# Layer 0's state turned between steps by DVE blocks and DMA through DRAM, with three smaller moves and a new rule of order, in a statically ordered graph kernel

## The chip, the cores and the metric

One core of a Trainium2 chip. Its engines are named as in the profile: PE is TensorE (products and transposes; PEld are its weight loads), DVE the vector engine, ACT the scalar engine, POOL is GpSimd, and SP (SyncE) issues the DMAs. PSUM is the memory that TensorE writes; ACT or DVE copies from there. The metric is device time of one execution in microseconds. The kernel before takes 1832.0 us (median of 4 runs, 1831.1 to 1833.3).

Ratios compare the mean time of one kernel's runs with the mean of the other's runs of the same rounds on the same chip, so they are not quite the ratio of the medians quoted beside them.

## The reference, cut

64 graphs of 256 nodes and 128 features, all float32, pass four layers, each with a residual and a layer norm. The parts that matter:

```python
# layer 0: a gated recurrent step, five times, with one adjacency matrix
def step(h, _):
    m_in = jnp.einsum('nm,bmd->bnd', in_matrix, h)          # needs h by nodes
    m_out = jnp.einsum('nm,bmd->bnd', out_matrix, h)
    av = jnp.concatenate([m_in, m_out], axis=-1)
    u3 = h @ u3_w.T + u3_b                                   # needs h by features
    z = jax.nn.sigmoid(av @ w3_w.T + w3_b + u3)
    r = jax.nn.sigmoid(av @ w4_w.T + w4_b + u3)
    hv = jnp.tanh(av @ w5_w.T + w5_b + (r * h @ u5_w.T + u5_b))
    h = (1.0 - z) * h + z * hv
# layer 2: attention; s_dst is needed as a row, the same on every partition
scores = s_src[:, :, None] + s_dst[:, None, :]
# every layer
x = _layernorm(x + layer(x), axis=-1)
```

A step makes the new state with features on partitions, and the next step's first product needs it with nodes on partitions as well. That turn, four times per pair of graphs, is what the change moves.

## The kernel before, the parts concerned

The kernel records every operation with its reads, writes, engine and an assumed duration. A list scheduler then fixes **one static order for each engine's queue** and assigns buffers. An engine waits at the head instruction of its queue, and what stands behind waits too: in the stall at 805 us below, a copy that ACT could have made from 803.6 us on was made at 806.59.

```python
SEEN = {"PE": 0.3, "ACT": 0.15, "DVE": 0.15, "POOL": 0.2, "SP": 2.5}
ABREAST = 4
...
# which ready operation comes next: earliest start, then oldest pair, then longest rest
key = (start + (us if len(op.ways) > 1 else 0.0), min(op.pair, self.n_pairs - ABREAST), -op.rest, op.number)
...
def transposes(i, x_like):                 # 4 TensorE transposes into PSUM
    ...
def to_sbuf(t, name):                      # PSUM copy, on ACT or DVE as the scheduler likes
    v = Value("A", name=name)
    evacuate(lambda: v.at(512), lambda: t.at(512), 0.6, 0.68, [t], [v])
    return v

def layer_norm(y, o):
    s, mv, rs = stats(y)                   # DVE statistics, then GpSimd: rs = (var + eps)**-0.5
    def fn():
        for c in range(4):
            nc.vector.tensor_scalar(tokens(o)[:, c, :], tokens(y)[:, c, :], mv()[:, c, 0:1], rs()[:, c:c + 1],
                                    op0=ALU.subtract, op1=ALU.mult)
    dve(1.4, fn, [y, s], [o])

def layer0(x0):
    hT = to_sbuf(transposes(x0, tokens), "hT")
    h = x0
    for s in range(STEPS):
        mT = to_sbuf(spread(h, aT), "mT")  # h is the stationary operand of this product
        ...                                # gates; the new state comes out as hT
        t = transposes(hT, lambda v: v.at(4, P))
        if s < STEPS - 1:
            h = to_sbuf(t, "h")

# layer 2: the score row, on every partition, by one 512-column product
pe(mm(512), lambda: nc.tensor.matmul(sd.at(512), vdst.ap, xT.at(512), start=True, stop=True), [vdst, xT], [sd])
```

## Time and profile before

| | before |
|---|---|
| time, median | 1832.0 us |
| TensorE busy | 1741 us, 95% |
| next engines | DVE 65%, ACT 43% |
| TensorE work by passes | 1700 us |
| not work: 0 to 200, 200 to 1600, from 1600 us on | 12, 50, 71 us |

"Work by passes" is the number of TensorE passes of each width times the start-to-start time of such a pass at full clock in the timeline (0.429 us for 512 columns, 0.216 for 256, 0.112 for 128, 0.110 for a transpose). What is left of a stretch is called its loss here: idle time, time at the halved clock, and passes that start later than they could. The lines are in the prediction.

### The profile page before, as it was taken

How to read it: one execution, taken by the hardware profiler on the slowest of the kernel's cores; microseconds unless marked ns; L12 is line 12 of the kernel's file. 1: busy time of each engine (PE TensorE's matmuls, PEld its weight loads, DVE VectorE, ACT ScalarE, POOL GpSimd, SP SyncE). 2: the span in 40 equal slices, each digit the busy share in tenths (PEclk: the TensorE clock that was granted, in tenths of full speed). 3: DMA queues.
4: the chain of work that ended last, by engine and by line, in shares of the span. 5: the costliest groups of instructions: out<-in, count | busy, mean ns of one | idle time of the engine just before them, and what ended most of it. 6: DMA issues, size and time to landing. Idle time of an engine off the chain costs nothing. (4 is left out here: it accounts for less than half of the span.)

```text
span 1832.3 us, 22228 instructions
## 1 busy us (share of the span) xinstructions
PE 1741.1 (95%) x7856; PEld 1230.3 (67%) x7856; DVE 1194.5 (65%) x3536; ACT 793.5 (43%) x1586; POOL 438.8 (24%) x519
## 2 busy tenths in 40 slices
PE   8999999999999999999999999999999999998767
PEld 6567576767767667676776666666766667665566
DVE  5466666667767667667776577665667666665753
ACT  3444445444445454434444444444444444443322
POOL 0022212312231221222222212231123222111152
PEclk9999999999999999999999999999999999999778
DMA  4000000000000000000000000000000000000000
GB/s 119 1 1 12 12 12 1 12 12 13 7 12 7 18 6 7 12 13 11 8 13 12 13 12 1 12 12 7 7 0 7 6 7 7 6 1 6 1 1 24
DMA packets 35024, 20.50 MB, mean 11 GB/s; under 512 B 1248, under 2 KB 34528, under 8 KB 34912
## 3 DMA queue, kind: packets, MB, share of 16 engines
q1 hardware_dynamic: 34912, 19.08, 3.6%
q8 instruction: 61, 1.00, 0.2%
q14 instruction: 51, 0.42, 0.1%
HBM read 10.69 MB, written 8.39 MB: 10 GB/s over the span
## 5 line engine op out<-in xcount | busy, mean ns | idle before, releaser
L173 ACT COPY a<-ps 128x512 f32<-128x512 f32 (+1 forms) x532 | 278.5, 541 | 483.5 <-PE ps L400 286.0
L419 POOL TENSOR_SCALAR s<-s 128x4 f32<-128x4 f32 x160 | 49.5, 310 | 986.1 <-DVE s L416 986.1
L400 PE MATMUL ps<-aT,a 128*128 128x256 f32 x1024 | 242.8, 379 | 1.7 <-ACT a L173 1.6
L400 PEld LDWEIGHTS ps<-aT,a 128*128 128x128 f32 x1024 | 189.9, 190 | 49.5 <-issue 24.5
L422 POOL TENSOR_TENSOR s<-s,neg_half 128x4 f32<-128x4 f32 x192 | 200.4, 1044 | 15.9
L430 DVE TENSOR_SCALAR x<-a,s 128x128 f32<-128x128 f32 x384 | 120.9, 370 | 100.1 <-POOL s L422 99.9
L462 DVE TENSOR_TENSOR a<-a,a 128x512 f32<-128x512 f32 x160 | 121.0, 756 | 95.4 <-ACT a L460 95.2
L460 ACT ACTIVATE a<-ps,bzrh 128x512 f32<-128x512 f32 x160 | 109.9, 687 | 160.6 <-PE ps L458 160.5
L446 ACT ACTIVATE a<-ps,bzrh 128x512 f32<-128x512 f32 x160 | 109.4, 685 | 160.1 <-PE ps L443 156.8
L448 DVE SCALAR_TENSOR_TENSOR a<-a,a 128x512 f32<-128x512 f32 x160 | 120.9, 759 | 81.1 <-ACT a L446 80.5
L414 DVE BATCH_NORM_STATS2 s<-a 128x6 f32<-128x128 f32 x640 | 141.5, 279 | 47.9 <-ACT a L173 45.7
L450 PE MATMUL ps<-a,w 128*128 128x512 f32 x320 | 163.0, 600 | 7.2 <-ACT a L446 7.0
L458 PE MATMUL ps<-a,u5h 128*128 128x512 f32 x320 | 164.4, 595 | 4.9 <-DVE a L448 4.9
L443 PE MATMUL ps<-a,w 128*128 128x512 f32 x320 | 163.6, 593 | 1.8 <-ACT a L173 1.8
L457 PE MATMUL ps<-a,w 128*128 128x512 f32 x320 | 164.5, 596 | 0.0
L442 PE MATMUL ps<-a,W 128*128 128x512 f32 x320 | 163.9, 594 | 0.0
L481 PEld LDWEIGHTS ps<-W,a 128*128 128x128 f32 x1024 | 131.7, 196 | 36.6 <-issue 17.9
L481 PE MATMUL ps<-W,a 128*128 128x128 f32 x1024 | 135.6, 281 | 8.7 <-DVE a L488 4.4
L452 ACT ACTIVATE a<-ps,bzrh 128x512 f32<-128x512 f32 x160 | 110.0, 688 | 62.7 <-PE ps L450 61.3
L400 PE MATMUL ps<-aT,x 128*128 128x256 f32 x512 | 129.3, 391 | 8.1 <-DVE x L430 7.7
L463 DVE SCALAR_TENSOR_TENSOR a<-a,a 128x512 f32<-128x512 f32 x160 | 118.5, 745 | 16.3 <-ACT a L452 13.9
L382 PEld LDWEIGHTS ps<-ident,a 128*128 128x128 f32 x768 | 92.4, 142 | 53.3 <-issue 23.2
(140 smaller groups left out, 2645.6 us busy)
## 6 DMA issues: line engine op xcount, KB each, us to landing
x<-x_in SPq DMA_DIRECT2D x32, 256.0 KB, 2.8
y_out<-a SPq DMA_DIRECT2D x32, 256.0 KB, 2.3
W<-mats_in SPq DMA_DIRECT2D x1, 832.0 KB, 6.7
W<-mats_in SPq DMA_DIRECT2D x1, 512.0 KB, 3.7
rbc<-rows_in SPq DMA_DIRECT2D x1, 385.0 KB, 7.2
aT<-adjT_in SPq DMA_DIRECT2D x1, 256.0 KB, 4.7
a<-adj_in SPq DMA_DIRECT2D x1, 256.0 KB, 5.9
ccol<-cols_in SPq DMA_DIRECT2D x1, 6.0 KB, 3.5
```

Of the source, the lines that this page charges most:

```text
L173: S.add([("ACT", us_act, lambda: nc.scalar.copy(o(), i())), ("DVE", us_dve, lambda: nc.vector.tensor_copy(o(), i()))], r, w)
L400: nc.tensor.matmul(t.at(2, N)[:, b, :], tokens(i)[:, 2 * b + j, :], right.ap[:, j, :], start=(j == 0), stop=(j == 1))
L414: nc.vector.bn_stats(st.at(4, 6)[:, c, :], tokens(y)[:, c, :])
L422: pool(1.04, lambda: nc.gpsimd.tensor_tensor(rs(), rs(), neg_half.ap, op=ALU.pow), [s, neg_half], [s])
L430: nc.vector.tensor_scalar(tokens(o)[:, c, :], tokens(y)[:, c, :], mv()[:, c, 0:1], rs()[:, c:c + 1], op0=ALU.subtract, op1=ALU.mult)
L442: nc.tensor.matmul(t.at(512), mat("u3"), hT.at(512), start=True, stop=False)
L443: nc.tensor.matmul(t.at(512), w345.ap[:, 1, :], mT.at(512), start=False, stop=True)
L450: pe(mm(512), lambda t=t, mT=mT: nc.tensor.matmul(t.at(512), w345.ap[:, 0, :], mT.at(512), start=False, stop=True, skip_group_check=True), ...
L457: nc.tensor.matmul(t.at(512), w345.ap[:, 2, :], mT.at(512), start=True, stop=False)
L458: nc.tensor.matmul(t.at(512), u5h.ap, r.at(512), start=False, stop=True)
L462: dve(0.7, lambda hv=hv, hT=hT: nc.vector.tensor_sub(hv.at(512), hv.at(512), hT.at(512)), [hv, hT], [hv])
L481: nc.tensor.matmul(tokens(t)[:, c, :], i.at(4, P)[:, c, :], w(), start=(k == 0), stop=(k == len(lefts) - 1))
```

## The change

The intent was to take everything from TensorE that is not arithmetic. In the words of its author, "the same, and layer 0's state is turned between its steps by DVE blocks and DMA through DRAM". Against the kernel before, the diff holds five things:

1. **Turn through DRAM**, for 28 of 32 pairs: DVE transposes 32x32 blocks, a store and four loads put the blocks in place. The spread then reads its weights at a step of four floats.
2. **First state arranged**: x is also loaded in its transposed layout (made on the host).
3. **Score row through DRAM**: a small DVE transpose and two DMAs in place of a product.
4. **Layer norms on ACT or DVE**, with one more small product on DVE between GpSimd and the normalizing.
5. **Order by deadlines**: 50 us apart, the last seven pairs 10 us apart.

Beside these the diff renews some assumed durations (2.5 to 3.3 us for a DMA, 0.70 to between 0.72 and 0.76 us for some DVE operations) and the numbers of buffers. Both bear on the order.

```diff
-SEEN = {... "SP": 2.5}
+SEEN = {... "SP": 3.3}
+DUE, LAST_DUE, LAST = 50.0, 10.0, 7
...
+    def tile(self, t):
+        return self.ap[:, t:512:4] if self.moved else self.ap[:, t * P:(t + 1) * P]
...
-                    key = (start + ..., min(op.pair, self.n_pairs - ABREAST), -op.rest, op.number)
+                    key = (start + ..., self.due(op.pair) - op.rest, op.number)
...
+        load(lambda: hTs[p].at(2, N), xT[2 * p:2 * p + 2].rearrange("b d n -> d b n"), hTs[p])
...
+    def turn_by_dma(i, name):
+        st, d, o = Value("A", name="turn"), Value("E", name="turn"), Value("A", name=name)
+        dve(1.11, lambda: nc.vector.transpose(st.ap.rearrange("p (b l t) -> p t b l", b=4, l=32), i.blocks()), [i], [st])
+        S.add([("SP", 0.45, lambda: nc.sync.dma_start(d.ap, st.ap))], [st], [d])
+        def move():
+            for f in range(4):
+                nc.sync.dma_start(o.ap[32 * f:32 * f + 32].rearrange("r (b n) -> r b n", b=4),
+                                  d.ap[:, f * P:(f + 1) * P].rearrange("(b r) n -> r b n", b=4))
+        S.add([("SP", 1.8, move)], [d], [o])
...
+        dve(0.16, lambda: nc.vector.scalar_tensor_tensor(nmr(), mv()[:, :, 0], -1.0, rs(), ...), [s], [s])
+        S.add([("ACT", 1.85, by_act), ("DVE", 1.45, by_dve)], [y, s], [o])
...
-            t = transposes(hT, lambda v: v.at(4, P))
-            if s < STEPS - 1:
-                h = to_sbuf(t, "h")
+            if s < STEPS - 1 and S.pair < n_pairs - BY_PE:      # BY_PE = 4
+                h = turn_by_dma(hT, "h")
+            else:
+                ...
...
-        pe(mm(512), lambda: nc.tensor.matmul(sd.at(512), vdst.ap, xT.at(512), ...), [vdst, xT], [sd])
+        dve(0.34, lambda: nc.vector.transpose(srow.at(4, 32), hs()[:, :, D - 30:D + 2]), [h], [srow])
+        S.add([("SP", 0.45, lambda: nc.sync.dma_start(line([32, 4], [P, 4], [1, 32]), srow.at(4, 32)[31::32]))], [srow], [d], 3.2)
+        S.add([("SP", 0.45, lambda: nc.sync.dma_start(sd.at(512), line([0, P], [1, 512])))], [d], [sd], 5.5)
```

## The prediction

> **What bounds the kernel now.** I read the page's busy shares first, then its slices, the windows of the steady part and of the end, TensorE's timeline, and its waits.
>
> ```profile
> span 1832.3 us, 22228 instructions
> PE 1741.1 (95%) x7856; PEld 1230.3 (67%) x7856; DVE 1194.5 (65%) x3536; ACT 793.5 (43%) x1586; POOL 438.8 (24%) x519
> PE   8999999999999999999999999999999999998767
> PEclk9999999999999999999999999999999999999778
> ```
>
> TensorE (PE) is busy 95% and the next engine, DVE, 65%. The row of slices shows one long saturated stretch and a bad end: in the last three or four slices of 46 us both the busy share and the granted clock fall.
>
> The windows of the steady part and of the end:
>
> ```profile
> 400.00:1600.00 1200.00, 1169.68 (x5338) 827.52 (x5337) 808.99 (x2379) 534.98 (x1067) 305.35 (x352) 1.00 0.03 9
> 1640.00:1690.00 50.00, 42.78 (x158) 26.48 (x156) 28.71 (x81) 19.54 (x32) 5.48 (x9) 0.97 0.02 6
> 1690.00:1760.00 70.00, 48.80 (x273) 41.23 (x274) 46.13 (x157) 25.38 (x73) 25.12 (x30) 0.77 0.00 1
> 1760.00:1833.00 73.00, 52.02 (x249) 44.58 (x247) 34.67 (x158) 15.96 (x32) 23.17 (x31) 0.83 0.05 15
> ```
>
> (Columns: stretch, length, busy of PE, PEld, DVE, ACT, POOL, granted clock, DMA share, GB/s.) Full-clock work in the last three is 42.78x0.97 + 48.80x0.77 + 52.02x0.83 = 122 us of 193, so **the end loses about 70 us**.
>
> A "mean ns" of a matmul is its latency, and matmuls overlap, so I take costs from start to start in TensorE's timeline:
>
> ```profile
> 810.97 1.04 PE L382 MATMUL ps<-ident,x 128*128 128x128 f32 x8
> 811.85 0.60 PE L382 MATMUL ps<-ident,a 128*128 128x128 f32 x4
> 812.28 1.02 PE L450 MATMUL ps<-a,w 128*128 128x512 f32 x2
> 813.14 0.59 PE L589 MATMUL ps<-vx,a 128*128 128x256 f32 x2
> ...
> 816.60 1.02 PE L510 MATMUL ps<-a,vdst 128*128 128x512 f32 x2
> 817.46 1.89 PE L597 MATMUL ps<-a,a2T 128*128 128x256 f32 x8
> ```
>
> Eight transposes start 0.88 us before the next group: **0.110 us each**. A 512-column product, which the trace holds as two passes, takes **0.86 us**. A 256-column product takes 0.43 us (two passes). 16 passes of 128 columns take 1.79 us elsewhere in the timeline, so 0.224 us a product.
>
> With the program's counts, before: 832 products of 512 (714 us), 1408 of 256 (608), 896 of 128 or 129 (200), 1544 transposes (170) and about 6 of setup, in all **1698 us of TensorE work**. The same count inside 400 to 1600 us gives 1154 of 1200 us: the steady stretch loses 3.8%. So 1698 + 3.8% of 1640 (62) + 70 at the end = 1830, which closes on the span. The waits of TensorE, summed over the whole run, are small except in the end, where one wait is 10.6 us:
>
> ```profile
> PE ps L400 <- DVE x L430: 14.3, 5, 6.6
> PE ps L382 <- DVE a L465: 11.5, 10, 2.3
> PE ps L284 <- ACT b L529: 10.6, 1, 10.6
> PE ps L400 <- DVE a L559: 7.0, 1, 7.0
> ```
>
> **What the Trainium skill says.** (1) "VectorE: DVE Perf Modes", The three transpose paths: DVE transposes only inside 32x32 blocks, TensorE a whole 128x128 into PSUM. That is why the change needs a DMA after the DVE instruction, to put blocks on other partitions. No run here has such an instruction yet.
> (2) "DMA: Bandwidth & Descriptors", Two DMAs through the same engine are not ordered: a DMA that reads what another wrote must wait for its completion semaphore. So the turn costs two whole landings in series. The trace has 2.3 us for a store and 2.8 us for a load of 256 KB.
> (3) "SBUF — State Buffer", Door 1 (the cacheline note): lines of 16 bytes, and each access on a new line pays a penalty. The turned state is read as weights at a step of 4 floats, exactly one line per element. The trace has only dense weight loads, 190 ns each; the penalty's size is open.
> (4) "TensorE: Matmul & The Clock Gate", Part 1: an idle window of about 3.4 us halves TensorE's clock. The trace agrees in kind: after the waits of 10.6 and 7.0 us the mean clock is 0.77.
>
> **The change part by part.**
>
> *Removed from TensorE.* The first state arrives already turned (a second load of x, arranged on the host): 32x4 transposes. The turn between steps leaves TensorE in steps 1 to 4 of 28 of the 32 pairs: 28x4x4 = 448. The program's order confirms it, 704+264 transposes instead of 1280+264: 576 x 0.110 = **-63.4 us**. In layer 2 the broadcast score row, a 512-column product per pair, becomes a small DVE transpose and two DMAs through DRAM: 32 x 0.86 = **-27.5 us**. The two score columns ride in the existing product, 130 columns instead of 129: nothing.
>
> *Added to TensorE.* 112 spreads of 1.72 us read their weights at the 16-byte step. A weight load of 190 ns hides under a pass of 215 ns, so it has 25 ns of slack. The diff's own scheduler charges these spreads 1.08; I take that as its author's estimate: 112 x 1.72 x 0.08 = **+15 us**. New work: 1698 - 63 - 27 + 15 = **1623 us**.
>
> *Other engines.* DVE gains 112 block transposes (about 1.1 us by the diff; the nearest row, a 128x512 DVE operation, is 0.75), 124 us, 32 small ones (11), and 160 more tiny multiplies of some 0.155 us (25). It loses 28 PSUM copies of 0.687 (19) and 344 of its normalizing operations of about 0.36 (124), which the scheduler gives to ACT. DVE: 1194 + 124 + 11 + 25 - 19 - 124 = 1211 us. ACT: 793 + 344x0.465 (160) - 116x0.587 (68) = 885 us. In a span of 1725 that is 70% and 51%; neither becomes the bound. SyncE issues 725 DMAs instead of 70; one issue measures 0.383 us, so 278 us, 16%.
>
> *Latency.* A turn was 0.44 us of PE and a copy of 0.59. It becomes 1.1 + 0.38 + 2.3 + 4 issues of 0.38 + 2.8 = about 8 us by the trace's figures, four times a pair; the score row adds some 6 us once. In the steady stretch the program keeps six to nine pairs in flight (from the order of its TensorE instructions), and gives 3.3 us to each landing, more than the trace shows. I expect it hidden: loss 4% instead of 3.8%, of about 1570 us: **63 us**.
>
> *The end.* Before, the last four pairs have equal priority and reach each stage together: in the timeline the 32 spread passes of four pairs follow one another, then all four wait on layer norm. After, deadlines are 50 us apart and 10 us for the last seven. By the program's order, in the last 41 us of TensorE work pairs 28, 29, 30 and 31 stand in different stages: layer 3 of 28 between layer 2 of 29 to 31. Only the last pair's end runs nearly alone. The last layer norm and store (10 us after the last matmul before) stay; the single waits of 6 to 10 us and most of the halved clock should go. I take **40 us** instead of 70: 10 for that last piece, about 20 for the gaps of pair 31's last chain, 10 for clock and small gaps.
>
> Sum: 1623 + 63 + 40 = 1726, stated as **1725 us**, 5.9% faster.
>
> **The rivals.** *Strided weights cost much more.* If a weight load at the 16-byte step took double, 380 ns, 896 passes would each lose 380 - 215 = 165 ns: 148 us instead of 15, and the time 1860, no gain. For it speaks the page's line rule; against it, that the author charges 8%, after durations which otherwise agree with the trace (0.00170 us a column against my 0.86/512 = 0.00168).
> *The turn's latency replaces the transpose as the wait.* Program order is fixed beforehand and SyncE's queue is in order, so one late DVE result holds up every later DMA. If every turn came 1 us too late for TensorE, 112 us would come back: about 1840. Against it: 8 us measured by parts beside 8.9 planned, and several pairs in flight. A partial form, 20 to 40 us, is quite possible, and it sets the upper side of my range.
> *The end keeps its loss.* With 70 us there: 1755. Ideal staggering, 25 us: 1710.
> *The transposes were hidden anyway.* No: they stand start to start in a saturated queue, so their time comes back one for one.
>
> **Range and chances.** Low: no stride cost, end at 30, steady loss as now: 1607 + 62 + 30 = 1699, with a little more for luck 1685. High: 15 of stride, 6% steady loss (95), end at 55: 1772. Range **1685 to 1775**. The limit for "faster by over 2%" is 1796, passed only if a rival takes 70 us more than planned: 0.93 faster, 0.05 within 2%, 0.02 slower.
>
> **What would show it.** TensorE instructions of about 7,216 (7856 - 576 - 64, a transpose being one pass); DVE near 1210 us, ACT near 885; the strided weight loads in the spread's group at 200 to 240 ns rather than 190; the turn's landings of 2 to 3 us; no large TensorE wait on DMA in the middle; clock of the last 140 us above 0.9. Wrong: weight loads near 380 ns, TensorE waiting on DMA for over 50 us in all, or steady busy under 94%.

## The result, and the profile after

The changed kernel took **1814.4 us** (1810.3 to 1815.3, 4 runs), ratio 0.990 with a 95% interval of 0.988 to 0.992: 1% faster where 5.9% was predicted, and far outside the range of 1685 to 1775.

The page of the changed kernel, the lines that answer to those of before:

```profile
span 1808.5 us, 22671 instructions
PE 1685.4 (93%) x7216; PEld 1206.1 (67%) x7216; DVE 1211.3 (67%) x3461; ACT 860.2 (48%) x1820; POOL 440.4 (24%) x519
PE   8999999998999999999999999999999999998886
PEclk9999999999999999999999999999999999999899
```

The busy sums came out nearly as predicted: 7216 TensorE instructions, DVE 1211 us, ACT 860 (885 predicted). Work by passes fell from 1700 to 1609 us. But TensorE's busy share fell as well. The work went and time did not follow. Windows of the steady part and of the end, the changed kernel (columns as in the prediction):

```profile
200.00:1600.00 1400.00, 1326.41 (x5637) 944.34 (x5636) 945.48 (x2660) 671.15 (x1410) 341.02 (x393) 0.99 0.17 53
1600.00:1808.00 208.00, 169.19 (x919) 137.64 (x917) 137.21 (x519) 104.78 (x257) 80.39 (x99) 0.94 0.06 17
```

and the kernel before:

```profile
200.00:1600.00 1400.00, 1367.41 (x6215) 964.82 (x6214) 934.69 (x2742) 627.75 (x1254) 347.66 (x402) 1.00 0.03 9
1600.00:1832.00 232.00, 183.20 (x833) 136.83 (x831) 134.30 (x454) 81.02 (x177) 60.39 (x75) 0.87 0.02 6
```

In 1400 steady us TensorE is idle for 73.6 us instead of 32.6. The end is better: mean clock 0.94 instead of 0.87.

The sum in the terms of the prediction, from the two traces:

| | before | after | effect on the time |
|---|---|---|---|
| work by passes | 1700 | 1609 | -91 |
| loss 0 to 200 us | 12 | 19 | +7 |
| loss 200 to 1600: strided weight loads | 0 | about 20 | +20 |
| loss 200 to 1600: all else | 50 | 105 | +56 |
| loss from 1600 on | 71 | 55 | -16 |
| span | 1832.3 | 1808.5 | -24 |

(The rows are rounded.) The 56 us in the middle are mostly two things: 41 us of new idle time and 12 us more lost to the halved clock, as counted below. Whom does TensorE wait for there? Its waits in the changed kernel, 200 to 1600 us (waiting line, releaser, us in total, times, longest):

```profile
PE ps L642 <- ACT a L192: 12.5, 6, 3.3
PE ps L529 <- ACT a L192: 9.4, 6, 3.8
PE ps L495 <- ACT a L491: 8.6, 9, 2.0
PE ps L402 <- DVE a L510: 8.4, 4, 3.0
PE ps L503 <- DVE a L493: 7.1, 4, 2.8
PE ps L488 <- ACT a L192: 5.6, 4, 3.0
```

Hardly once does TensorE wait for a DMA (0.4 us in the whole run, beside one wait for the first load). It waits for ACT: PSUM copies (L192) and tanhs (L491). All TensorE waits of this stretch sum to 74 us, 48 of them on ACT and 25 on DVE; before it was 32, with 13 on ACT. And ACT is busy only 48%. What does ACT wait for? The same stretch, ACT:

```profile
ACT x L473 <- DVE s L462: 68.4, 33, 6.3
ACT a L603 <- POOL a L602: 61.5, 18, 5.9
ACT a L473 <- DVE s L462: 57.0, 33, 5.2
ACT b L579 <- DVE s L571: 45.0, 21, 4.9
```

L473 is the layer norm on ACT and L462 is the new small product on DVE: 125 us of waiting at the head of ACT's queue (the kernel before had 37 us, at its one layer norm on ACT). L579 is layer 2's first activation, behind the score row; its counterpart before waited 19 us for DVE. L603 is layer 2's ReLU, behind GpSimd.

How much of TensorE's 74 us hangs on these heads can be read from the trace: from each wait to the instruction that ended it, and on that engine back through instructions that ran without a pause to the last one that had stood waiting. 23 us lie behind ACT's layer norms (21 waits), 15 behind the ReLU, 14 behind the small product itself, which stands in DVE's queue for GpSimd, and 8 behind L579. Before, the ReLU stood for 9, layer norms on DVE for 8, the one on ACT for 1, the first activation for 2.

One stall shows how a queue's head holds TensorE up. Timeline of the changed kernel around 805 us: DVE, ACT, then TensorE.

```profile
802.32 1.29 DVE L565 TENSOR_TENSOR b<-a,maskb 128x512 f32<-128x512 f32 x2 [0.46 <-DMA a<-d]
803.53 0.69 DVE L507 TENSOR_TENSOR a<-a,a 128x512 f32<-128x512 f32 x1
804.13 1.22 DVE L571 TENSOR_REDUCE s<-b 128x4 f32<-128x1024 f32 x1
```

```profile
801.89 0.37 ACT L192 COPY a<-ps 128x256 f32<-128x256 f32 x1 [1.04 <-DVE a L421]
805.38 1.31 ACT L579 ACTIVATE b<-b,h 128x256 f32<-128x256 f32 x3 [3.12 <-DVE s L571]
806.59 0.35 ACT L192 COPY a<-ps 128x256 f32<-128x256 f32 x1
```

```profile
804.35 0.59 PE L642 MATMUL ps<-a,a2T 128*128 128x256 f32 x2
806.99 2.56 PE L642 MATMUL ps<-a,a2T 128*128 128x256 f32 x6 [2.05 <-ACT a L192]
809.35 2.62 PE L438 MATMUL ps<-offT,x 128*128 128x256 f32 x8
811.80 0.60 PE L402 MATMUL ps<-ident,x 128*128 128x128 f32 x4
```

DVE waits 0.46 us for the score row from DRAM, does its additions, another operation and the reduction. ACT stands 3.12 us at the activation that needs the reduction; only 0.46 us of that is the row's wait. The PSUM copy behind it, for another pair, had been possible since its product ended at 803.6 us, but comes after three of these activations in ACT's order. TensorE waits 2.05 us for that copy. Then it pays again: 6 passes take 2.36 us from start to start instead of 1.29, and the next 8 take 2.45 instead of 1.73. In this trace's clock records the clock is halved for 3.4 us just there. Between 200 and 1600 us there are ten such halved intervals, 17 us lost; before there were three, 5 us.

The strided weight loads, too, can be read in TensorE's timeline. Eight passes of a turned state against eight dense ones:

```profile
830.38 2.14 PE L438 MATMUL ps<-aT,a 128*128 128x256 f32 x8
832.36 1.02 PE L487 MATMUL ps<-t,W 128*128 128x512 f32 x2
...
846.17 1.89 PE L438 MATMUL ps<-offT,x 128*128 128x256 f32 x8
847.90 0.60 PE L402 MATMUL ps<-ident,x 128*128 128x128 f32 x4
```

1.98 us against 1.73. Over all passes of that group the trace gives a median of 234 ns from one to the next where dense ones give 216, and about 335 where the first load is not hidden; together some 20 us. The strided loads themselves take about 330 ns each.

### The profile page after: what moved, and what is told of

Read it like the earlier page. It is cut to its first block, busy times and chain, and to the rows that moved or that the text cites. A ratio compares the mean times of both kernels' runs of the same rounds, so it can differ in the third digit from the quotient of the medians.

```text
span 1808.5 us, 22671 instructions
## 1 busy us (share of the span) xinstructions
PE 1685.4 (93%) x7216; PEld 1206.1 (67%) x7216; DVE 1211.3 (67%) x3461; ACT 860.2 (48%) x1820; POOL 440.4 (24%) x519
## 5 line engine op out<-in xcount | busy, mean ns | idle before, releaser
L192 ACT COPY a<-ps 128x512 f32<-128x512 f32 (+1 forms) x422 | 215.3, 520 | 292.4 <-PE ps L438 189.5
L457 POOL TENSOR_SCALAR s<-s 128x4 f32<-128x4 f32 x160 | 53.5, 334 | 948.6 <-DVE s L454 853.6
L438 PEld LDWEIGHTS ps<-aT,a 128*128 128x128 f32 x1024 | 248.9, 309 | 33.6 <-issue 18.5
L438 PE MATMUL ps<-aT,a 128*128 128x256 f32 x1024 | 266.4, 401 | 1.4 <-ACT a L192 1.0
L462 DVE SCALAR_TENSOR_TENSOR s<-s 128x4 f32<-128x4 f32 x192 | 38.5, 201 | 206.3 <-POOL s L460 206.1
L491 ACT ACTIVATE a<-ps,bzrh 128x512 f32<-128x512 f32 x160 | 108.9, 682 | 136.9 <-PE ps L488 135.9
L473 ACT ACTIVATE x<-a,s 128x128 f32<-128x128 f32 x248 | 107.9, 485 | 97.3 <-DVE s L462 97.3
L507 DVE TENSOR_TENSOR a<-a,a 128x512 f32<-128x512 f32 x128 | 93.3, 729 | 72.1 <-ACT a L505 72.0
L493 DVE SCALAR_TENSOR_TENSOR a<-a,a 128x512 f32<-128x512 f32 x128 | 89.7, 703 | 64.7 <-ACT a L491 64.1
L487 PE MATMUL ps<-a,W 128*128 128x512 f32 x256 | 131.1, 594 | 1.4 <-DVE h L555 1.3
L508 DVE SCALAR_TENSOR_TENSOR a<-a,a 128x512 f32<-128x512 f32 x160 | 120.0, 752 | 18.1 <-ACT a L497 15.5
```

What stands on the lines that cost most here:

```text
L192: S.add([("ACT", us_act, lambda: nc.scalar.copy(o(), i())), ("DVE", us_dve, lambda: nc.vector.tensor_copy(o(), i()))], r, w)
L438: nc.tensor.matmul(t.at(2, N)[:, b, :], i.tile(2 * b + j), right.ap[:, j, :], start=(j == 0), stop=(j == 1))
L487: nc.tensor.matmul(t.at(512), mat("u3"), hT.at(512), start=True, stop=False)
L508: dve(0.74, lambda hv=hv, z=z: nc.vector.scalar_tensor_tensor(hv.at(512), z.at(512), 1.0, hv.at(512), op0=ALU.add, op1=ALU.mult), [hv, z], ...
```

## The experiments

Eighteen runs, in rounds against the kernel before (1831 to 1833 in each). "Steady" is TensorE's loss between 200 and 1600 us, and "work" the work by passes, both from the profiled run. That run is one of several and not always a typical one: it lies 4 to 10 us below the median in after, e6, e7 and c4, and 5 above it in e2. In e7 the runs at 1754 and 1757 us had a mean clock of 0.993 and more, the four at 1764 to 1767 one of 0.988 or 0.989; so its 66 belongs to a run 10 us faster than the median. The medians decide.

| run | what | median us | ratio | work | steady |
|---|---|---|---|---|---|
| before | | 1832.0 | 1 | 1700 | 50 |
| after | all five parts | 1814.4 | 0.990 | 1609 | 126 |
| e4_before_new_order | before + deadlines | 1795.8 | 0.981 | 1700 | 45 |
| e3_old_order | after, old order | 1835.2 | 1.001 | 1609 | 134 |
| e1_turn_on_pe | after, turns on TensorE | 1831.8 | 1.000 | 1658 | 97 |
| e2_dense_weights | after, dense weights (wrong values) | 1807.8 | 0.988 | 1609 | 128 |
| e5_row_on_pe | after, row on TensorE | 1797.0 | 0.981 | 1636 | 102 |
| e6_norm_on_dve | after, layer norms as before | 1774.0 | 0.968 | 1609 | 88 |
| e7_row_and_norm | both of these ("mended") | **1764.5** | 0.964 | 1636 | 66 |
| e8_turn_alone | mended, first state by TensorE | 1793.1 | 0.979 | 1651 | 82 |
| e9_dve_norm_product_kept | after, norms on DVE, product kept | 1799.0 | 0.982 | 1609 | 105 |
| e10_e7_turns_on_pe | mended, turns on TensorE | 1804.2 | 0.985 | 1686 | 55 |
| e11_e7_dense_weights | mended, dense (wrong values) | 1751.2 | 0.956 | 1636 | 59 |
| e12_e7_no_block_transpose | mended, no DVE transposes (wrong values) | 1749.2 | 0.955 | 1636 | 57 |
| c1_after_48, c2_after_52 | after, other deadlines | 1816.2, 1807.5 | 0.991, 0.987 | 1609 | 129, 123 |
| c3_mended_48, c4_mended_52 | mended, other deadlines | 1778.5, 1772.1 | 0.970, 0.967 | 1636 | 80, 73 |
| e13_act_norm_no_wait | after, ACT's norm reads a constant (wrong values) | 1781.5 | 0.972 | 1609 | 96 |
| e14_row_no_wait | after, row read from a constant (wrong values meant) | 1788.0 | 0.975 | 1609 | 113 |

### First round: turn or order?

Theory T: the turn's longer way loosens the steady stretch. Rival O: the new order does.

**e1.** `-BY_PE = 4` / `+BY_PE = 32`

> The changed kernel with all 128 turns between steps on TensorE (BY_PE = 32, so 112 come back); the rest of the change stays. TensorE's work counted by passes rises by 112 x 0.44 = 49 us to 1653 us, and no weight load is strided any more (about -20 us). Theory T (the turn through DRAM is what loosens the steady stretch: of 200 to 1600 us the changed kernel loses 124 us, the kernel before 48): the loss falls back to about 50 and the time is 1775 to 1795, faster than the changed kernel. Rival O (the new order and the other parts loosen it): the loss stays near 100 and the time is 1830 to 1845, slower than the changed kernel.

1831.8 us. T falls: with no turn through DRAM at all the steady loss is still 97, and 20 of the fall from 126 is the stride. The time is what O foretold.

**e2.** `-return self.ap[:, t:512:4] if self.moved else self.ap[:, t * P:(t + 1) * P]` / `+return self.ap[:, t * P:(t + 1) * P]`

> The changed kernel, but the spreads read the turned state as if it were dense (values wrong on purpose, same instructions, same DMAs, same order). In the changed kernel a strided pass starts 234 ns before the next one, a dense one 216, and some first passes 335: 896 passes make some 20 us. If the stride costs only that, the time falls by 15 to 25 us to about 1792; if it also upsets the order of the engines, by 30 us or more; if it is hidden, by under 8.

1807.8 us, 6.6 less by the medians and 4 by the ratios, the branch "hidden". In the traces the order of TensorE, ACT, DVE and GpSimd is the same instruction by instruction. The passes did get shorter (the loss holds no stride any more), yet in the profiled runs the steady loss stayed at 128, TensorE's idle time rose from 74 to 84 us, and the halved clock cost 26 us instead of 17. These two runs overstate it: the changed kernel's was its fastest, e2's its slowest. By medians or ratios at most a third of the 20 us came back; **most of the time taken from TensorE turned into waiting and halved clock**.

**e3.** The deadline key replaced by the old one: `-self.due(op.pair) - op.rest` / `+min(op.pair, self.n_pairs - 4), -op.rest`

> The changed kernel with the old rule of order (oldest pair first, the last four alike, then the longest rest) in place of deadlines; nothing else. Rival O (the deadline order is what loosens the steady stretch): loss in the steady stretch falls by some 40 us, the end gets some 15 us worse, time 1785 to 1795. Theory T: the steady loss stays above 110, the end gets worse, time 1820 to 1835.

1835.2 us, as T had it, though T was already out. O falls: the old order does not mend the middle.

**e4.** The kernel before with `-min(op.pair, self.n_pairs - ABREAST), -op.rest` / `+self.due(op.pair) - op.rest`

> The kernel before with only the rule of order exchanged for the deadlines (50 us apart, 10 for the last seven). Work unchanged at 1693 us by passes. If the new order costs nothing in the middle and mends the end: 1832 - 17 to 25 = 1807 to 1815. Rival O: the middle loses some 40 us more: 1850 or above.

1795.8 us, below the 1807 to 1815 expected: **36 us faster from the order alone**, more than the whole change gave. Its losses: middle 45, end 36 instead of 71. The windows of the end (from 1600 us on; those of before and after are above):

```profile
1600.00:1793.00 193.00, 165.98 (x908) 132.78 (x906) 145.00 (x539) 80.36 (x192) 81.23 (x98) 0.97 0.04 10
```

Both of my theories were wrong, and the round says more than they did: the order is worth 36 us, and the other parts together, which take 91 us of work from TensorE, cost 19 us net on top of it.

### Second round: which part?

New theories: S, the score row's way; N, the layer norms shared with ACT. The waits of ACT above had pointed at both.

**e5.** The row's DVE transpose and DMAs taken out, the product put back:

```diff
-        dve(0.34, lambda: nc.vector.transpose(srow.at(4, 32), ...), [h], [srow])
-        S.add([("SP", 0.45, ...)], [srow], [d], 3.2)
-        S.add([("SP", 0.45, ...)], [d], [sd], 5.5)
+        pe(mm(512), lambda: nc.tensor.matmul(sd.at(512), vdst.ap, xT.at(512), start=True, stop=True), [vdst, xT], [sd])
```

> After the first four runs: the new order alone takes 36 us off the kernel before, and the changed kernel with all turns on TensorE gives all of that back. So some other part loosens the steady stretch. Here the changed kernel with layer 2's score row made by TensorE again (no small DVE transpose, no two DMAs through DRAM); TensorE's work rises 27 us. Theory S (the row's way through DRAM is what loosens it): steady loss falls by 40 to 50 us, time 1788 to 1800. Otherwise the work comes on top: 1830 to 1842.

1797.0 us, within S's range: 17 us faster with 27 us more work. But the steady loss fell by 24, not by the 40 to 50 of the theory; 13 more came at the end, whose loss is 42 instead of 55.

**e6.** `layer_norm` and layer 2's middle norm put back as in the kernel before.

> The changed kernel with the layer norms as in the kernel before (always on DVE, straight after GpSimd, no extra small product; layer 2's middle one on ACT). TensorE's work unchanged. Theory N (layer norms on ACT put its queue behind DVE's and GpSimd's results, and TensorE then waits for ACT's PSUM copies): the steady loss falls by 40 to 50 us, time 1765 to 1778. Otherwise 1808 to 1820.

1774.0 us, as theory N had it: **40 us** with TensorE's work unchanged, though DVE now has more to do (1027 us in the steady stretch against 945) and ACT less.

**e7.** Both.

> The changed kernel with both undone, score row on TensorE and layer norms on DVE; the turn through DRAM and the arranged first load stay. TensorE's work rises 27 us. Theory S or N: 1785 to 1800. Theory T (the turn itself loosens it): about 1840.

1764.5 us (six runs, 1754 to 1767), the fastest correct kernel, 20 us below the range of S or N; T's 1840 is out. TensorE's waits in the steady stretch sum to 33 us, as before the change, 14 of them on ACT; the loss of the end is 36. Its window:

```profile
200.00:1600.00 1400.00, 1367.15 (x5859) 974.02 (x5858) 1012.07 (x2848) 602.73 (x1203) 350.18 (x409) 1.00 0.16 49
```

**e8.** e7, and the first state turned by TensorE: `-load(... hTs[p] ...)` / `+hT = turn(x0, "hT")`

> As the run before, and the first state turned by TensorE again: the new order and the turn through DRAM alone. Work by passes 1604 + 27 + 14 = 1645 us, strided loads some 22. If the turn is harmless: losses as with the new order alone (head 20, steady 43, end 36) give 1766 to 1780. Theory T: 1795 or above. If the arranged first load is what hurts, this run is faster than the run before it in spite of 14 us more work.

1793.1 us, in neither range, 29 more than e7 for 14 us of work. So the turn beside the new order alone gained next to nothing over e4 (1795.8), which spoke for T again in a weaker form.

### Third round: what of the norms, what is the turn worth?

**e9.** `-S.add([("ACT", 1.85, by_act), ("DVE", 1.45, by_dve)], ...)` / `+S.add([("DVE", 1.45, by_dve)], ...)`

> The changed kernel (1814) with one way struck out: layer norms on DVE only, but the new small product (minus mean times 1/sigma) stays on DVE ahead of each. Undoing the layer norm part whole gave 1774. If it is ACT's queue standing behind the product that loosens the stretch, nearly all of the 40 us come back: 1772 to 1785. If it is the extra product on DVE: little comes back, 1800 to 1815.

1799.0 us: 15 of the 40 us. Neither answer. This run loads DVE's queue with the norms and the product (and with layer 2's middle norm, which e6 had put back on ACT), so it does not single out one wait. In its trace 27 us of TensorE's steady waits lie behind the product in DVE's queue, so the product costs there as well. That is why e13 was made.

**e10.** e7 with `-BY_PE = 4` / `+BY_PE = 32`

> The kernel with score row on TensorE and layer norms on DVE (1764), and all turns on TensorE: the new order and the arranged first load alone. Work by passes 1636 + 49 = 1685 us, no strided load. If the turn through DRAM pays in this mended kernel what its passes say (49 less about 20 for the stride): 1790 to 1797. If the turn is worth nothing, as between the new order alone and the new order with the turn (1796 and 1793): 1762 to 1770.

1804.2 us, slower than either range: in the mended kernel the turn is worth 40 us, more than the 29 that its passes say. With e1 (17) and e8 against e4 (3) that makes three very different answers for the same part.

**e11.** e7 with the edit of e2.

> The same mended kernel (1764) with the turned state read as if dense (values wrong on purpose). In the changed kernel this gave 4 us of the 20 that the passes show. If TensorE's work is again what bounds the mended kernel: 1742 to 1750. If the queues of the other engines bound it as well: 1757 to 1763.

1751.2 us, just above the first range: 13 us. In the same order as e7 (the traces agree instruction by instruction), two thirds of the 20 us now reach the time, where the changed kernel gave at most a third.

**e12.** e7 with `-dve(1.11, lambda: nc.vector.transpose(...), [i], [st])`, and the store reading `i` instead of `st`.

> The same mended kernel (1764) without DVE's 112 block transposes; the store takes the state as it is (values wrong on purpose). 124 us of DVE work (7% of the span) and one step of each turn less, TensorE's work unchanged. If DVE's load by the turn is what keeps TensorE waiting: 1740 to 1752. If not: 1758 to 1766.

1749.2 us: 15 us, within the first range. It suggests that DVE's part of the turn costs time, though DVE is busy only 72% of the mended kernel's steady stretch. But the edit changes the order too and takes a step from each turn, and the controls below show differences of 14 us from order alone, so this is not shown.

### Controls: how much is the luck of one order?

Nearly every edit reshuffles the static order (e2 and e11 do not). The controls keep the operations, but for some copies that change between ACT and DVE, and change only the deadlines, `DUE = 50.0` to 48 or 52.

> Control of luck: the changed kernel with deadlines 48 us apart in place of 50. The same instructions in another order. If the costs found so far belong to the parts of the change: 1805 to 1822, like the changed kernel. If they are luck of one order: it may fall to 1780 or below.

> The same control with 52 us. Parts: 1805 to 1822. Luck: 1780 or below.

> The mended kernel (score row on TensorE, layer norms on DVE, 1764) with deadlines 48 us apart. Parts: 1755 to 1775. Luck of one order: 1790 or above.

> The same with 52 us. Parts: 1755 to 1775. Luck: 1790 or above.

1816.2 and 1807.5 for the changed kernel (1814.4 at 50), 1778.5 and 1772.1 for the mended one (1764.5 at 50; the first came out above the 1775 of its expectation). One order differs from another by up to 14 us, but the two groups stay 29 us apart at their nearest. The means of the three are 41 us apart, so the parts cost some 40 us net of the 27 us of work that the mended kernel takes back. The traces agree: in the steady stretch of all three changed kernels 20 to 23 us of TensorE's waits lie behind ACT's layer norms, in the mended ones none. Differences below some 15 us between kernels of different order prove nothing. What the arranged first load is worth is not settled either: e7, which has it, is 29 us faster than e8, which has not; but e10, which has it too, is 8 us slower than e4, which has not and does 14 us more work.

### Last round: take one wait away, keep the plan

These two change what one instruction reads, not what is declared to the scheduler. Its plan stays, but by the traces the order on the engines does not quite: compared as sequences, some 45 of TensorE's 7216 instructions, 280 of ACT's 1820 and 65 of DVE's 3461 stand elsewhere in e13, none of ACT's by more than 20 places; in e14 some 55, 440 and 500.

**e13.** In ACT's layer norm: `-bias=nmr()[:, c:c + 1], scale=rs()[:, c:c + 1]` / `+bias=neg_half.ap[:, c:c + 1], scale=neg_half.ap[:, c:c + 1]`

> The changed kernel; only ACT's layer norm instructions take scale and bias from a constant (values wrong on purpose), so ACT no longer waits there for DVE's product and GpSimd's power. Number of instructions and, but for local swaps, the order stay. ACT waited 125 us at these instructions in the steady stretch of the changed kernel. Theory N' (this wait in ACT's in-order queue delays the PSUM copies and tanhs behind it, and so TensorE): 1785 to 1798. If ACT's wait costs nothing: 1808 to 1818.

1781.5 us, below the range of 1785 to 1798: **33 us**. In its steady stretch ACT no longer waits for the product. The longest waits of ACT are now for TensorE; at L473 it still stands some 105 us, but mostly for the norm's own input or its statistics:

```profile
ACT a L192 <- PE ps L438: 139.8, 117, 6.1
ACT a L505 <- PE ps L503: 121.4, 82, 7.2
ACT a L491 <- PE ps L488: 109.1, 83, 7.5
ACT a L603 <- POOL a L602: 55.2, 18, 5.9
...
ACT x L473 <- DVE a L541: 33.4, 12, 5.3
ACT a L473 <- DVE s L452: 25.6, 12, 3.4
```

So the sum of ACT's waits hardly tells what they cost; who stands behind does. TensorE's waits fall from 74 to 53 us, and those behind ACT's layer norms from 23 to 5, while those behind the ReLU (15 and 15), L579 (8 and 8) and DVE's product (14 and 18) stay. That points at ACT's queue and not at the shorter chain of the pair itself, which this edit brings as well.

**e14.** In layer 2's two additions: `-sd.at(512)[:, None, ...]` / `+rbc.ap[:, None, ...]`

> The changed kernel; only the two additions of layer 2 read a constant row in place of the row that came through DRAM (values wrong on purpose; the DVE transpose and both DMAs stay). DVE waited 23 us there in the steady stretch. If the wait for the row is the row's cost: 1785 to 1800. If its cost is the longer way that the plan must give it: 1806 to 1818.

1788.0 us: **26 us** by the medians. The wait that the edit takes away is, in the changed kernel:

```profile
DVE b L565 <- DMA a<-d: 22.9, 13, 4.7
```

The small DVE transpose and both DMAs still run, and the scheduler's plan is the same. So it is the reading of the row, not the longer way in the plan, that costs. How it costs is less clear than in e13: without that wait the additions also move in DVE's order, TensorE's steady waits fall only from 74 to 65 us (those behind L579 from 8 to 1, those behind the next activation, L582, rise from 1 to 5), and the loss falls by 13 us in the middle and 6 at the end. (The result still passed the comparison with the reference; the row's share in the output lies within the tolerance. Correctness is therefore no evidence about this row.)

## Why the prediction was wrong

- **Work taken from TensorE**: right. 1609 us by passes plus 20 for the stride, against 1623.
- **Strided weights**: the 15 us were near; the passes show about 20. That was luck: loads of 200 to 240 ns were predicted, and they took mostly 330. By the prediction's own rule, load less pass, that would have cost 896 x (330 - 215) = 103 us. The rule failed, since these loads overlap one another: eight of them fill 1.95 us in the trace, not 2.64. So the rival's long loads nearly came, and its cost did not.
- **Other engines**: the busy sums were right (DVE 1211 against 1211, ACT 860 against 885; of DMAs 726 were issued, not 725), and the inference failed. "70% and 51%; neither becomes the bound" took the share of busy time for freedom. A queue that stands at one head instruction held up what lay behind it, in ACT at 48% busy. The prediction had this thought among its rivals, but for SyncE's queue and the turn.
- **Latency, "I expect it hidden: loss 4%"**: this is the step that failed. 4% of the 1400 steady us is 56 us; the loss measured there was 126, of which 20 are stride. The prediction's own sign, steady busy under 94%, would have missed it: busy was 94.7%, with the idle time more than doubled. I had looked for the danger in the turn's 8 us. The DMAs of the turn are indeed hidden: TensorE waited 0.4 us for them. The waits came from two parts that I had dismissed in half a sentence each. "160 more tiny multiplies" were counted as 25 us of DVE work, and 344 normalizing operations as work moved to ACT; their effect was layer norms that stood in ACT's queue behind one more step of two other engines, 33 us by e13, 40 by e6. The score row, "adds some 6 us once", cost 26 us by e14; with it on TensorE again the time fell by 17 us in spite of 27 us more work (e5). Ten of the stalls brought a halved clock as well. I had ACT's PSUM copies in view only as work removed from ACT, not as what TensorE would wait for.
- **The end**: the mechanism was right. Staggering took 35 us from the end when alone (e4: 71 to 36). In the changed kernel it left 55, against 40 predicted. The same two parts make the difference: the traces give 42 with the row undone (e5), 48 with the norms (e6), and 36 with both (e7).
- **"Their time comes back one for one"**: wrong in the changed kernel. With the order kept, of 20 us of TensorE time 4 to 7 came back there (e2) and 13 in the mended kernel (e11).
- **What stays open**: the worth of the turn by itself (17, 40 and 3 us in three settings), that of the arranged first load, and how the 40 us of the layer norms divide between ACT's wait and the extra product. In e13 and e14 instructions swapped places, so a part of their 33 and 26 us, by the controls up to some 10, may be luck. No run takes both waits away at once, so whether the two add up is not shown. The mended kernel lost far less time (at 50 us of deadline it is 50 us faster with 27 us more work), but it also has other orders, fewer DMAs and less on ACT.

## What to carry to other kernels

In a kernel whose queues have a fixed order, count for each moved operation not only its busy time but **whose queue will stand behind its input**, and which copies for the bounding engine lie behind it there. Work may leave the bounding engine and still cost time, if it goes by a step that makes a half-idle engine wait at its head. Change the rule of order by itself first: here it gave twice the gain of the whole change. And before believing a difference of under 1% between two static orders, reshuffle the order without changing anything else; look also whether the one run that was profiled is a typical one.

## What the Trainium skill lacked or had wrong

- "SBUF — State Buffer", Door 1: the page says that each access on a new 16-byte line pays, without a size. For float32 weights at a step of 16 bytes the loads took mostly 330 ns instead of 190, and a pass of 256 columns 234 ns instead of 216, since most of the load is hidden; some 20 us over 896 passes.
- "VectorE: DVE Perf Modes", The three transpose paths: it has 311 ns for a 128x128 bf16 transpose and nothing for float32. Here a 128x128 float32 one took 305 ns, and a 128x512 one with an output step of 16 bytes 1.11 us.
- "TensorE: Matmul & The Clock Gate", Part 1: the window of about 3.4 us and the half rate agree with the trace, but an idle time shorter than a window can be enough: after an idle time of 2.05 us the clock was halved for 3.4 us, which cost 1.8 us more. It need not be: in the same trace idle times of 3.33 and 3.76 us passed without.
- No page that I used says what a wait of a lightly loaded engine costs the bounding one: taking one wait of ACT (48% busy) away gave 33 us of 1814, one of DVE (67% busy) 26 us, up to some 10 of which may be the changed order.
